# Gated graph layers by row halves, tiny VectorE operations with two tensors, and new durations for the merge

## The chip, the cores and the metric

The kernel runs on one core of a Trainium2 chip. The metric is the device time of one execution in microseconds (us). A run here is a median of several executions, taken on one chip together with executions of the kernel before. Views of the profile, and losses per period, come from one profiled execution of each kernel. A *ratio* is the mean time of one kernel's fast executions over that of the kernel before in the same rounds, so it is not quite the quotient of the two medians beside it.

## The reference, cut to what matters

`x` has shape (128, 64, 256): 128 graphs of 64 nodes. Four graph layers follow one another, each `x = layernorm(x + layer(x, adj))`. Two of them matter here.

```python
# layer 0: five gated steps
A = (adj != 0).astype(x.dtype)
for l in range(5):
    m = einsum('bnd,de->bne', h, weight[l])
    agg = einsum('bij,bid->bjd', A, m)
    h = gru_cell(agg, h, w_ih, w_hh, b_ih, b_hh)   # r, z, n; h' = (1-z)*n + z*h
# layer 2: norm and logarithm of each row, then the graph sum, then back onto the ball
n = clip(norm(x), 1e-15); x_tangent = arctanh(clip(n)) * x / n
support = einsum('bij,bjd->bid', adj, x_tangent)
out = project(tanh(norm(support)) * support / norm(support))
```

## The kernel before

The 128 graphs are 16 groups of 512 rows; three groups are in flight. Every operation is first *recorded* with an engine, a cost in us, what it writes and what it reads. A greedy merge then fixes the order in which the operations of the groups in flight are issued, so the order is static and depends on the recorded costs (`HOPS` is the time that it allows for a result to reach another engine):

```python
HOPS = {"from PE": 0.3, "to PE": 0.4, "else": 0.2}
def dve(n, run, w, r):  flow.op("DVE", 0.16 + 0.0011 * n, run, w, r)
def act(n, run, w, r):  flow.op("ACT", 0.16 + 0.001 * n, run, w, r)
def pool(us, run, w, r=()):  flow.op("POOL", us, run, w, r)
```

Each gated layer makes 512 x 256 products in two halves of 256 rows with fewer multiplications than the plain way. It needs four differences, t1 to t4, that GpSimd computes and that TensorE then multiplies by prepared weights:

```python
minus(t1, of(a, 1), of(a, 0), [a])                    # a is agg; of(a, n) is its half n
minus(t2, of(h, 1), lambda: view(t1), [(h, 1), t1])
minus(t3, of(h, 1), of(a, 1), [(h, 1), (a, 1)])
minus(t4, lambda: view(t2), of(h, 0), [t2, (h, 0)])
... # p_hn with 512 columns
product(p1, a11[l], k_of(a, 0), True, False, (a, 0))
act(512, copy of p1 to uu)                            # the "U copy"
product(p_in[0], ...); product(p1, a12, ...); tanh; new_n(0, ur)
product(pu, s2[l], k_view(t2), True, True, t2);  plus(uu, pu, uu)
product(pw, s1[l], k_view(t1), True, True, t1);  plus(uw, pw, uu)
product(pv, s3[l], k_view(t3), True, False, t3); plus(uz, pv, uw)
product(p4, s4[l], ...)
... # tanhs, p_in[1], new_n(1), then pv += na22 * t4, new_state(1), new_state(0)
```

`plus` is an addition on VectorE of a PSUM bank (pu, pv, pw and the other banks take the products' results) and an SBUF tile. In the profile t1 and t2 are the halves of tile tA, t3 and t4 those of tB; U, V, Z and R hold the sums, hT the state, and x_n is the layer norm's output, made from mv, ve and rstd. In layer 2 the norm's square root is a `pow` on GpSimd, the limits and the logarithm's argument `fac` are a chain of VectorE operations on 128x4, and `Ln` is on ScalarE.

## Time and profile before

| | before |
|---|---|
| time, median of 3 (range) | 2674.82 us (2669.52 to 2675.11) |
| TensorE busy | 93% of the span |
| matmul work at back-to-back spacing | 2405 us |
| steady period of a group | 159.2 us |
| of it lost on TensorE (gaps and slow matmuls) | 10.7 us |

The order repeats from group to group, so the steady period (start of one group's `ps_hid` to the next one's) is the thing to compare. A period's loss is the sum over its matmuls of the distance to the next matmul, less the distance that the same width has back to back (0.216 us at 256 columns).

### The profile page before, as it was taken

How to read it: one execution, taken by the hardware profiler on the slowest of the kernel's cores; microseconds unless marked ns; L12 is line 12 of the kernel's file. 1: busy time of each engine (PE TensorE's matmuls, PEld its weight loads, DVE VectorE, ACT ScalarE, POOL GpSimd, SP SyncE). 2: the span in 40 equal slices, each digit the busy share in tenths (PEclk: the TensorE clock that was granted, in tenths of full speed). 3: DMA queues.
4: the chain of work that ended last, by engine and by line, in shares of the span. 5: the costliest groups of instructions: out<-in, count | busy, mean ns of one | idle time of the engine just before them, and what ended most of it. 6: DMA issues, size and time to landing. Idle time of an engine off the chain costs nothing.

```text
span 2673.3 us, 31183 instructions
## 1 busy us (share of the span) xinstructions
PE 2491.5 (93%) x11330; PEld 1963.8 (73%) x11330; DVE 1606.5 (60%) x3593; ACT 1068.0 (40%) x2211; POOL 746.1 (28%) x707
## 2 busy tenths in 40 slices
PE   8999899999999999999999999999999999999874
PEld 5877777678677777877778687777877777777643
DVE  2456666466574756756476575646657575566635
ACT  2444343344343434434344443434434443433322
POOL 4232232322314132132413313232132413222220
PEclk9999999999999999999999999999999999999887
DMA  3000000000000000000000000000000000000000
GB/s 117 1 9 0 18 9 11 16 1 26 1 19 9 1 26 1 18 9 18 9 1 26 1 19 8 11 17 1 26 1 18 8 1 26 1 9 8 8 8 8
DMA packets 39144, 35.07 MB, mean 13 GB/s; under 512 B 9892, under 2 KB 38592, under 8 KB 38992
## 3 DMA queue, kind: packets, MB, share of 16 engines
q1 hardware_dynamic: 34848, 28.05, 3.4%
q10 hardware_dynamic: 3744, 4.46, 0.5%
q8 instruction: 90, 1.47, 0.2%
q0 software_dynamic: 400, 0.57, 0.1%
q14 instruction: 62, 0.51, 0.1%
HBM read 24.69 MB, written 8.39 MB: 12 GB/s over the span
## 4 chain that ended last, share of the span: by engine, by line
PE 49%; issue 19%; DVE 14%; POOL 13%; ACT 4%; DMA 0%; POOLq 0%; DVEq 0%; ACTq 0%
PE ps_o L222 8%; PE ps_hid L222 8%; PE p_r L480 7%; POOL tA L537 5%; PE p_v L480 4%; POOL tB L537 4%; PE p_hn L222 4%; PE ps_agg L222 3%; PE p_w L480 3%; PE p_in L480 3%; PE p_u L480 3%; POOL rstd L492 2%; PE ps_a L222 2%; DVE st L489 1%; DVE x_n L495 1%
## 5 line engine op out<-in xcount | busy, mean ns | idle before, releaser
L537 POOL TENSOR_TENSOR tA<-agg 128x512 f32<-128x512 f32 x80 | 107.3, 1341 | 900.3 <-ACT agg L474 620.3
L480 PE MATMUL p_in<-agg,w_in 128*128 128x256 f32 x1280 | 310.9, 382 | 0.0
L222 PE MATMUL p_hn<-hT,w_hn 128*128 128x512 f32 x640 | 306.6, 598 | 0.1
L480 PEld LDWEIGHTS p_in<-agg,w_in 128*128 128x128 f32 x1280 | 243.2, 192 | 31.8
L222 PE MATMUL ps_o<-w2s,hid 128*128 128x256 f32 x1024 | 231.0, 381 | 5.9 <-DVE hid L690 5.9
L222 PE MATMUL ps_hid<-aggm,w1s 128*128 128x512 f32 x512 | 224.6, 597 | 0.7 <-ACT aggm L474 0.7
L222 PEld LDWEIGHTS ps_o<-w2s,hid 128*128 128x128 f32 x1024 | 195.1, 191 | 40.8 <-DVE hid L690 7.9
L670 DVE TENSOR_TENSOR sqs<-sqs,sq 128x512 f32<-128x512 f32 x112 | 79.1, 706 | 225.0 <-POOL sq L667 224.7
L480 PE MATMUL p_r<-hT,a 128*128 128x256 f32 x640 | 176.5, 419 | 37.4 <-ACT U L601 37.4
L480 PEld LDWEIGHTS p_r<-hT,a 128*128 128x128 f32 x640 | 133.8, 212 | 69.7 <-ACT U L601 43.5
L222 PEld LDWEIGHTS ps_hid<-aggm,w1s 128*128 128x128 f32 x512 | 97.8, 192 | 118.1 <-issue 115.4
L561 ACT ACTIVATE hnb<-p_hn,half_b 128x512 f32<-128x512 f32 x160 | 109.7, 686 | 151.5 <-PE p_hn L222 151.4
L222 PEld LDWEIGHTS p_hn<-hT,w_hn 128*128 128x128 f32 x640 | 114.9, 192 | 74.3 <-issue 66.7
L583 DVE SCALAR_TENSOR_TENSOR R<-R,hnb 128x512 f32<-128x512 f32 x80 | 54.9, 686 | 190.2 <-ACT R L574 190.2
L480 PE MATMUL p_u<-tA,s 128*128 128x256 f32 x640 | 164.2, 391 | 0.0
L480 PE MATMUL p_r<-agg,a 128*128 128x256 f32 x640 | 157.5, 379 | 0.0
L480 PE MATMUL p_r<-hT,s 128*128 128x256 f32 x640 | 155.9, 379 | 0.0
L495 DVE TENSOR_SCALAR x_n<-y,mv,rstd 128x256 f32<-128x256 f32 x192 | 66.4, 408 | 148.6 <-POOL rstd L492 148.6
L480 PE MATMUL p_v<-tB,s 128*128 128x256 f32 x640 | 154.4, 381 | 0.0
L480 PEld LDWEIGHTS p_r<-agg,a 128*128 128x128 f32 x640 | 119.4, 190 | 47.5 <-issue 32.7
L480 PE MATMUL p_w<-tA,s 128*128 128x256 f32 x640 | 153.8, 379 | 0.0
L480 PE MATMUL p_v<-tB,na 128*128 128x256 f32 x640 | 153.8, 379 | 0.0
(179 smaller groups left out, 4837.2 us busy)
## 6 DMA issues: line engine op xcount, KB each, us to landing
x<-in_x_dram SPq DMA_DIRECT2D x16, 512.0 KB, 4.1
xr<-in_x_dram SPq DMA_DIRECT2D x16, 512.0 KB, 3.9
out_dram<-x_n SPq DMA_DIRECT2D x16, 512.0 KB, 2.9
edge<-in_adj_dram SPq DMA_DIRECT2D x32, 64.0 KB, 2.4
wm<-in_L_gnn_weight_dram ACTq DMA_DIRECT2D x5, 256.0 KB, 8.4
w1s<-in_L_gnn_W_dram ACTq DMA_DIRECT2D x1, 1024.0 KB, 11.5
w2s<-in_L_gnn_W_dram ACTq DMA_DIRECT2D x1, 1024.0 KB, 9.2
aw_in_L_gnn_w_ih_dram<-in_L_gnn_w_ih_dram ACTq DMA_DIRECT2D x1, 512.0 KB, 6.1
```

The lines of the kernel that those rows point to most:

```text
L222: nc.tensor.matmul(o, lhsT, rhs, start=(k == 0), stop=(k == nk - 1))
L480: pe(256, lambda c=c, k=k: nc.tensor.matmul(ps[:, c * HR:(c + 1) * HR], w[:, k, c * P:(c + 1) * P], v(k), start=first and c == k == 0, sto ...
L489: dve(256, lambda b=b: nc.vector.bn_stats(st[:, b, :], y[:, b, :]), [(st, b)], [(y, b)])
L492: pool(1.04, lambda: nc.gpsimd.tensor_tensor(rstd.tile(), ve.tile(), m_half, OP.pow), [rstd], [ve])
L495: dve(256, lambda b=b: nc.vector.tensor_scalar(o[:, b, :], y[:, b, :], mv[:, b, 0:1], rstd[:, b:b + 1], OP.subtract, OP.mult), [(o, b)], [ ...
L537: pool(1.04, lambda: nc.gpsimd.tensor_sub(view(o), x0(), x1()), [o], r)
L561: act(512, lambda ps=ps, c=c, hnb=hnb: nc.scalar.activation(hnb[:, c, :], ps.tile(), AF.Identity, bias=half_b[:, 2 * KD + c:2 * KD + c + 1 ...
L583: dve(512, lambda: nc.vector.scalar_tensor_tensor(t.tile(), t.tile(), 1.0, hnb[:, :, half(n)], OP.add, OP.mult), [t], [t, hnb])
L670: dve(512, lambda sq=sq: nc.vector.tensor_add(sqs.tile(), sqs.tile(), sq.tile()), [sqs], [sqs, sq])
```

## The change

The intent: half 0 of a gated layer should end early, the durations that the merge uses should be those of the trace, and tiny VectorE operations should escape waiting for GpSimd. Cut to the core:

```diff
-    HOPS = {"from PE": 0.3, "to PE": 0.4, "else": 0.2}
+    HOPS = {"from PE": 0.25, "to PE": 0.3, "else": 0.1}
-        flow.op("DVE", 0.16 + 0.0011 * n, run, w, r)
+        flow.op("DVE", 0.16 + 0.00105 * n, run, w, r)
-        flow.op("ACT", 0.16 + 0.001 * n, run, w, r)
+        flow.op("ACT", 0.27 + 0.00077 * n, run, w, r)
-                pool(1.04, lambda: nc.gpsimd.tensor_sub(view(o), x0(), x1()), [o], r)
+                pool(1.32, lambda: nc.gpsimd.tensor_sub(view(o), x0(), x1()), [o], r)
 ...
+            def sides(n):          # turn, aggregate and p_hn of half n
+                ...
+            sides(0)
             product(p1, a11[l], k_of(a, 0), True, False, (a, 0))
 ...
             new_n(0, ur)
+            sides(1)
+            minus(t1, ...); minus(t2, ...); minus(t3, ...); minus(t4, ...)
             product(pu, s2[l], k_view(t2), True, True, t2)
             plus(uu, pu, uu)
+            product(pv, s3[l], k_view(t3), True, False, t3)
+            plus(uv, pv, uu)
+            product(pw, s1[l], k_view(t1), True, False, t1)
+            product(pv, na22, k_view(t4), False, True, t4)
+            plus(uv, pw, uv)
+            plus(uz, pv, uu)
+            product(pw, s4[l], k_of(h, 1), False, True, (h, 1))
 ... # new_state(0) as soon as uz is there; half 1 last
-        dve(4, lambda: nc.vector.tensor_scalar(xn.tile(), xn.tile(), MIN_NORM, None, OP.max), [xn], [xn])
+        dve(4, lambda: nc.vector.scalar_tensor_tensor(xn.tile(), xn.tile(), MIN_NORM, xn.tile(), OP.max, OP.max), [xn], [xn])
 ... # eight more of this kind
```

So there are three parts: **tiny** (two tensors), **durations**, and **halves**.

More of the change, by code (lines that the diff above doesn't have):

```diff
@@ L275 @@
     nc.vector.memset(ones, 1.0)
+    one4 = const.tile([P, NB], F32, name="one4")
+    nc.vector.memset(one4, 1.0)
     p_half = const.tile([P, NB], F32, name="p_half")
@@ L395, in sums @@
                 flow.op(e, us, lambda o=o, x0=x0, x1=x1: v.tensor_sub(o.tile(), x0.tile(), x1.tile()), [o], [x0, x1])
-        sums("DVE", 0.7) if l == 0 else sums("POOL", 1.04)
+        sums("DVE", 0.7) if l == 0 else sums("POOL", 1.32)
     load(1)
@@ L521, in gated @@
             hr = rows("B", f"hr{l}") if l else xt
-            for n in range(2):
+            hnb = u("y", f"hnb{l}", (P, KD, R))
+            def sides(n):
                 if l:
                     ps = rows_of(h, n)
-                    act(512, lambda ps=ps, n=n: nc.scalar.copy(hr[:, 2 * n:2 * n + 2, :], blocks_of(ps.tile())),
+                    act(512, lambda: nc.scalar.copy(hr[:, 2 * n:2 * n + 2, :], blocks_of(ps.tile())),
                         [(hr, 2 * n), (hr, 2 * n + 1)], [ps])
                 aggregate(agg, hr, 2 * n, n)
+                p_hn = bank("p_hn")
+                product(p_hn, w_hn, lambda k: h[:, k, half(n)], True, True, (h, n))
+                for c in range(KD):
+                    act(300, lambda c=c: nc.scalar.activation(
+                        hnb[:, c, half(n)], p_hn[:, c * HR:(c + 1) * HR], AF.Identity,
+                        bias=half_b[:, 2 * KD + c:2 * KD + c + 1], scale=0.5), [(hnb, (n, c))], [p_hn, half_b])
             hN = u("h", f"hT{l}", (P, KD, R))
@@ L546, in k_view @@
                 return lambda k: t[0][:, t[1] * KD + k, :]
-            minus(t1, of(a, 1), of(a, 0), [a])
-            minus(t2, of(h, 1), lambda: view(t1), [(h, 1), t1])
-            minus(t3, of(h, 1), of(a, 1), [(h, 1), (a, 1)])
-            minus(t4, lambda: view(t2), of(h, 0), [t2, (h, 0)])
-            hnb = u("y", f"hnb{l}", (P, KD, R))
-            for c in range(KD):
-                ps = bank("p_hn")
-                for k in range(KD):
-                    pe(512, lambda ps=ps, c=c, k=k, h=h: matmul(
-                        ps.tile(), w_hn[:, k, c * P:(c + 1) * P], h[:, k, :], k, KD), [ps], [w_hn, h])
-                act(512, lambda ps=ps, c=c, hnb=hnb: nc.scalar.activation(
-                    hnb[:, c, :], ps.tile(), AF.Identity, bias=half_b[:, 2 * KD + c:2 * KD + c + 1], scale=0.5),
-                    [(hnb, c)], [ps, half_b])
-            p1, pu, pv, pw, p4 = bank("p_r0"), bank("p_u"), bank("p_v"), bank("p_w"), bank("p_r1")
+            p1, pu, pv, pw = bank("p_r0"), bank("p_u"), bank("p_v"), bank("p_w")
             p_in = [bank("p_in"), bank("p_in")]
-            uu, uw, uz, ur = (u(t, f"{t}_{l}", (P, KD, HR)) for t in "UVZR")
+            uu, uz, uv, ur = (u(t, f"{t}_{l}", (P, KD, HR)) for t in ("ZUVR" if l % 2 else "UZVR"))
             def plus(o, ps, x):
@@ L583, in new_n @@
                 dve(512, lambda: nc.vector.scalar_tensor_tensor(
-                    t.tile(), t.tile(), 1.0, hnb[:, :, half(n)], OP.add, OP.mult), [t], [t, hnb])
+                    t.tile(), t.tile(), 1.0, hnb[:, :, half(n)], OP.add, OP.mult), [t], [t, (hnb, (n, 0)), (hnb, (n, 1))])
                 dve(512, lambda: nc.vector.tensor_add(t.tile(), blocks_of(p_in[n].tile()), t.tile()), [t], [t, p_in[n]])
@@ L596, in new_state @@
                     hN[:, :, half(n)], hN[:, :, half(n)], 0.5, t.tile(), OP.mult, OP.add), [(hN, n)], [(hN, n), t])
+            sides(0)
             product(p1, a11[l], k_of(a, 0), True, False, (a, 0))
-            act(512, lambda: nc.scalar.copy(uu.tile(), blocks_of(p1.tile())), [uu], [p1])
+            act(420, lambda: nc.scalar.copy(uu.tile(), blocks_of(p1.tile())), [uu], [p1])
             product(p_in[0], w_in[l], k_of(a, 0), True, True, (a, 0))
@@ L605, in gated @@
             new_n(0, ur)
+            sides(1)
+            minus(t1, of(a, 1), of(a, 0), [a])
+            minus(t2, of(h, 1), lambda: view(t1), [(h, 1), t1])
+            minus(t3, of(h, 1), of(a, 1), [(h, 1), (a, 1)])
+            minus(t4, lambda: view(t2), of(h, 0), [t2, (h, 0)])
             product(pu, s2[l], k_view(t2), True, True, t2)
             plus(uu, pu, uu)
-            product(pw, s1[l], k_view(t1), True, True, t1)
-            plus(uw, pw, uu)
             product(pv, s3[l], k_view(t3), True, False, t3)
-            plus(uz, pv, uw)
-            product(p4, s4[l], k_of(h, 1), True, True, (h, 1))
-            plus(uw, p4, uw)
-            tanh_half(uw, inplace(uw), 0, uw)
+            plus(uv, pv, uu)
[4 more added lines that the diff above has]
+            product(pw, s4[l], k_of(h, 1), False, True, (h, 1))
             tanh_half(uz, inplace(uz), 1, uz)
+            new_state(0, ur, uz)
+            tanh_half(uv, inplace(uv), 1, uv)
+            plus(uu, pw, uu)
             product(p_in[1], w_in[l], k_of(a, 1), True, True, (a, 1))
-            new_n(1, uw)
-            product(pv, na22, k_view(t4), False, True, t4)
-            plus(uu, pv, uu)
-            tanh_half(uu, inplace(uu), 1, uu)
-            new_state(1, uw, uz)
-            new_state(0, ur, uu)
+            tanh_half(uu, inplace(uu), 0, uu)
+            new_n(1, uu)
+            new_state(1, uu, uv)
             return hN
@@ L714, in group @@
         pool(1.04, lambda: nc.gpsimd.tensor_tensor(xn.tile(), ss.tile(), p_half, OP.pow), [xn], [ss])
-        dve(4, lambda: nc.vector.tensor_scalar(xn.tile(), xn.tile(), MIN_NORM, None, OP.max), [xn], [xn])
+        dve(4, lambda: nc.vector.scalar_tensor_tensor(xn.tile(), xn.tile(), MIN_NORM, xn.tile(), OP.max, OP.max), [xn], [xn])
         dve(4, lambda: nc.vector.reciprocal(rn.tile(), xn.tile()), [rn], [xn])
-        dve(4, lambda: nc.vector.tensor_scalar(xn.tile(), xn.tile(), MAX_ARG, None, OP.min), [xn], [xn])
-        dve(4, lambda: nc.vector.tensor_scalar(fac.tile(), xn.tile(), -1.0, 1.0, OP.mult, OP.add), [fac], [xn])
+        dve(4, lambda: nc.vector.scalar_tensor_tensor(xn.tile(), xn.tile(), MAX_ARG, xn.tile(), OP.min, OP.min), [xn], [xn])
+        dve(4, lambda: nc.vector.scalar_tensor_tensor(fac.tile(), xn.tile(), -1.0, one4, OP.mult, OP.add), [fac], [xn])
         dve(4, lambda: nc.vector.reciprocal(fac.tile(), fac.tile()), [fac], [fac])
@@ L727, in series @@
             nc.vector.tensor_mul(n2.tile(), xn.tile(), xn.tile())
-            nc.vector.tensor_scalar(ser.tile(), n2.tile(), 1.0 / 13.0, None, OP.mult)
+            nc.vector.scalar_tensor_tensor(ser.tile(), n2.tile(), 1.0 / 13.0, one4, OP.mult, OP.mult)
             for q in (11, 9, 7, 5, 3):
                 nc.vector.scalar_tensor_tensor(ser.tile(), ser.tile(), 1.0 / q, n2.tile(), OP.add, OP.mult)
-            nc.vector.tensor_scalar(ser.tile(), ser.tile(), 1.0, None, OP.add)
-            nc.vector.tensor_scalar(near.tile(), xn.tile(), SERIES_BELOW, None, OP.is_lt)
+            nc.vector.tensor_add(ser.tile(), ser.tile(), one4)
+            nc.vector.scalar_tensor_tensor(near.tile(), xn.tile(), SERIES_BELOW, one4, OP.is_lt, OP.mult)
         dve(1250, series, [n2, ser, near], [xn])
@@ L754, in group @@
         pool(1.04, lambda: nc.gpsimd.tensor_tensor(un.tile(), us.tile(), p_half, OP.pow), [un], [us])
-        dve(4, lambda: nc.vector.tensor_scalar(unb.tile(), un.tile(), MIN_NORM, None, OP.max), [unb], [un])
+        dve(4, lambda: nc.vector.scalar_tensor_tensor(unb.tile(), un.tile(), MIN_NORM, un.tile(), OP.max, OP.max), [unb], [un])
         act(64, lambda: nc.scalar.activation(th.tile(), unb.tile(), AF.Tanh), [th], [unb])
@@ L761, in onto_ball @@
             nc.vector.tensor_mul(un.tile(), th.tile(), un.tile())
-            nc.vector.tensor_scalar(un.tile(), un.tile(), MIN_NORM, None, OP.max)
+            nc.vector.scalar_tensor_tensor(un.tile(), un.tile(), MIN_NORM, un.tile(), OP.max, OP.max)
             nc.vector.reciprocal(un.tile(), un.tile())
-            nc.vector.tensor_scalar(un.tile(), un.tile(), MAX_NORM, 1.0, OP.mult, OP.min)
+            nc.vector.scalar_tensor_tensor(un.tile(), un.tile(), MAX_NORM, one4, OP.mult, OP.min)
             nc.vector.tensor_mul(th.tile(), th.tile(), un.tile())
```

## The prediction

> **What bounds the kernel now.** I read the page's busy line and slices first, then the stretches table, then TensorE's timeline over two group periods, then the other engines' timelines where TensorE waited.
>
> The page, busy times and slices:
> ```profile
> PE 2491.5 (93%) x11330; PEld 1963.8 (73%) x11330; DVE 1606.5 (60%) x3593; ACT 1068.0 (40%) x2211; POOL 746.1 (28%) x707
> ...
> PE   8999899999999999999999999999999999999874
> ```
> TensorE is the bound from end to end; only the last slices fall off. How near is it to gapless? In the timeline back-to-back matmuls start 0.216 us apart at 256 columns, 0.430 at 512 and about 0.110 at 128. All 11330 records at these spacings make 2405 us. The first matmul starts at 10.8 us and the last ends at 2664.0, so 2664 - 10.8 - 2405 = 248 us are lost in between: 77 us after 2480, where fewer groups are left; about 29 before 480; some 140 in the 13 steady group periods of 160 us, 10.5 us each. No reordering can win more than the steady 140 us (5.2%) plus a part of the ends.
>
> Two stalls recur in every period. TensorE's timeline around each:
> ```profile
> 1052.64 1.89 PE L480 MATMUL p_in<-agg,w_in 128*128 128x256 f32 x8
> 1057.28 2.67 PE L480 MATMUL p_r<-hT,a 128*128 128x256 f32 x8 [2.74 <-ACT U L601]
> ...
> 991.06 1.46 PE L480 MATMUL p_in<-agg,w_in 128*128 128x256 f32 x6
> 995.59 2.45 PE L222 MATMUL ps_agg<-edge,x_n 128*128 128x128 f32 x16 [3.07 <-DVE x_n L495]
> ```
> Eight matmuls take 1.89 us, but 2.67 or more after the stall: matmuls come every 0.427 us for some 4 us before 0.216 returns. So the first stall costs 2.9 + 9 x 0.21 = 4.8 us, the second 3.2 + 1.3 = 4.5. With 0.8 us at ps_a and up to 0.9 at ps_hr that is the 10.5. Stalls of 0.9 us leave no slow matmuls behind, nor does one of 2.3 us at 479; one of 2.4 at 443 does.
>
> The second stall is a queue on GpSimd. Its timeline:
> ```profile
> 992.41 1.26 POOL L537 TENSOR_TENSOR tB<-tA,hT 128x512 f32<-128x512 f32 x1
> 993.64 0.23 POOL L491 TENSOR_SCALAR ve<-mv 128x4 f32<-128x4 f32 x1
> 993.96 1.04 POOL L492 TENSOR_TENSOR rstd<-ve,m_half 128x4 f32<-128x4 f32 x1
> ```
> The layer norm's mv was ready at 988.2; its ve stood behind eight subtractions of two groups. The first stall: ScalarE stands in Ln from 1050.8 to 1056.0, waiting for fac, and the copy U that TensorE needs stands behind it. fac is late because of tiny VectorE operations:
> ```profile
> 1050.86 1.22 DVE L715 TENSOR_SCALAR n<-n 128x4 f32<-128x4 f32 x1 [2.65 <-POOL n L714]
> 1052.12 0.18 DVE L716 RECIPROCAL rn<-n 128x4 f32<-128x4 f32 x1
> 1052.33 0.98 DVE L717 TENSOR_SCALAR n<-n 128x4 f32<-128x4 f32 x1
> ```
> The 1.22 and 0.98 end when GpSimd's current subtraction ends; in the last group, with GpSimd idle, the same lines take 0.17.
>
> **What the Trainium skill says.** "SBUF — State Buffer", SBUF: two separate sides: VectorE and GpSimd share one port pair, an exclusive lock, taken by a VectorE operation in a 2-port mode *or with two SBUF inputs*; the loser blocks. The trace agrees on both halves, and this matters, for the change gives the tiny operations two SBUF inputs. At 2484.7 GpSimd runs a subtraction:
> ```profile
> 2484.67 1.27 POOL L537 TENSOR_TENSOR tB<-tA,hT 128x512 f32<-128x512 f32 x1
> 2484.73 1.23 DVE L727 TENSOR_TENSOR n<-n 128x4 f32<-128x4 f32 x1
> 2485.88 0.16 DVE L732 TENSOR_SCALAR near<-n 128x4 int32<-128x4 f32 x1
> ```
> L727 has two tensor inputs and takes 1.23 instead of 0.15. Likewise L595 (two SBUF inputs, 128x512) takes about 1.75 us in the 19 cases that start inside a subtraction and 0.68 elsewhere. "TensorE: Matmul & The Clock Gate", Part 1: a window of about 3.4 us without work halves TensorE's clock until it has been busy that long. The trace agrees in kind; here gaps of 2.4 to 3.2 us already do it. "PSUM — Partial Sum Buffer", Engine vs sequencer instructions: ScalarE, VectorE and GpSimd queues are strict FIFO; the two stalls above are that.
>
> **The change part by part.**
>
> *p_hn by halves.* 4 matmul pairs of 512 columns a layer become 8 of 256: 8 x 0.430 = 3.44 us against 16 x 0.216 = 3.46. Over 80 layers +1.6 us. Weight loads (0.19 us each) fit under a 0.216 matmul. ScalarE's hnb goes from two of 0.686 to four of about 0.47, +0.5 us a layer, 40 us of an engine that is 40% busy: not on the path by itself.
>
> *Same products, same sums.* Nine products of 4 matmul pairs and five additions a layer, before and after. Total TensorE work is 2407 us.
>
> *Tiny operations.* Nine of a group's TENSOR_SCALARs get two tensors. If that escaped the lock, L715, L717, L719 and L728 would lose about 0.77 us each, fac would come 3.5 us sooner, and the first stall (16 x 4.8 = 77 us at most) would go. By L727 it does not escape; what decides is whether GpSimd is busy then. I count nothing for the replacement itself.
>
> *The new order* decides. I compared the built instruction orders of both kernels. First, both old stalls: the U copy now precedes Ln on ScalarE or belongs elsewhere, and at most one group's four subtractions stand before the layer norm's ve. With durations from the trace x_n arrives 1 to 2 us before its matmuls. Both stalls go: -9.3 us a group.
>
> Second, what it adds. The differences t1..t4 need both halves of agg. Before, all of half 0's products ran after agg: in the steady groups the order has 6.9 to 9.5 us of matmuls (counted at the spacings above) between the last ps_agg of layers 2 to 4 and p_u. Now half 1's agg comes after half 0's products, and mostly 3.9 to 5.8 us is left. p_u needs t2, the third subtraction: 0.2 hop + 0.58 copy + 3 x 1.22 + 0.15 = 4.6 us. So many layers stall by 0 to 0.7 us. In every second group (7, 9, 11, 13) layer 3 has only 1.3 us: a stall of 3.3 us, with slow matmuls 5.2.
>
> The order repeats every two groups. I followed the queues by hand through both kinds of period from the end of ps_o. Odd group under way: agg2's copy stands behind a Square that waits for x_n, so p_u waits 1.8; tan is 1.3 late; the copy of agg0 stands behind a Tanh, p_in waits 1.7; p_u of layer 0 0.7; small ones 0.7; layer 3 5.2. Sum 11.4 us. Even: p_r behind the same Square 1.1; x3T behind Tanhs 1.0; ps_e behind gated VectorE work 1.9; ps_T and layer 4 0.9. Sum 4.9 us. Mean 8.2, to which port blocking adds: GpSimd's fours now fall beside new_state and beside the tiny chain before y2, 1 to 3 us a group. New: about 10 us against 10.5.
>
> The ends: in the last group's layers half 1's chain (two Tanhs, five VectorE operations, 6 us) now follows the last matmul, where before 3.6 us were waited; earlier layers win about 2 each from the early half 0. Together -3 us. Sum: 13 x (10.0 - 10.5) - 3 + 1.6 = -8 us. I allow for some of my waits overlapping and take -15: 2660 us.
>
> **Rivals.** (1) *The old stalls go and little replaces them.* For it: VectorE and ScalarE are idle 40% and 60%, and the scheduler's GpSimd figure (1.32 instead of 1.04) now is close to the measured 1.27. Against: p_u's distance of 1.3 us is in the order. It would make 2674 - 13 x 6 - 5 = 2590 us. (2) *The tiny operations do escape the lock.* Against: L727. If GpSimd is idle in their place it hardly matters; where it is busy (before y2) it saves up to 2 us a group: 2635 us. (3) *More stalls cross the length that halves the clock.* Each costs about 2 us more; with two more a group +50 us: 2710 us. (4) *ScalarE becomes the wait*, having 42 more us and Ln in its queue: contained in my counts, else as (3).
>
> **Range and chances.** Of the hand-followed waits each may be off by 1 us, so a period by perhaps 3 us, 13 x 3 = 39 us around 2660, cut at the upper side by what the order still has to interleave: 2618 to 2704. Faster by over 2% (below 2621) needs rival 1 nearly in full: 0.15. Slower by over 2% (above 2728): 0.05. Within: 0.80.
>
> **What would show it.** Right, if TensorE's busy work is unchanged (11970 records, 640 more), waits for ACT U and for x_n at ps_agg have nearly gone, and p_u waits for GpSimd's tA in the odd groups with slow matmuls behind it, p_in for ACT agg. The tiny lines: 0.17 us where GpSimd is idle, over 1 us for two-tensor forms that start inside a subtraction. Wrong, if steady periods fall below 155 us (the added waits do not occur), or if two-tensor tiny operations stay at 0.17 beside a running subtraction.

## More of the kernel before

The waits in total, from the list of what TensorE waited for (columns: tile and line, what released it and its line, us in total, times, longest):

```profile
PE ps_agg L222 <- DVE x_n L495: 43.0, 15, 4.6
PE p_r L480 <- ACT U L601: 37.4, 14, 4.1
PE ps_hr L461 <- DVE hT L595: 22.0, 18, 4.9
```

The first two are the stalls that the prediction describes.

## The result, and the profile after

After: 2712.54 us median of 4 (2706.25 to 2713.96); before in the same rounds 2674.87. The ratio is 1.0141, with a 95% interval of 1.0120 to 1.0162. The change makes the kernel 38 us slower.

The page of the changed kernel, busy times and TensorE's slices:

```profile
PE 2488.3 (92%) x11970; PEld 2059.1 (76%) x11970; DVE 1675.7 (62%) x3594; ACT 1079.3 (40%) x2371; POOL 780.8 (29%) x707
...
PE   7999998999999899998999989999999999999874
```

There are 640 more matmul records, as expected, and no more TensorE work. VectorE is 69 us busier than before (1606.5) although it does the same operations (one constant is set in addition). What TensorE waited for:

```profile
PE p_u L482 <- POOL tA L550: 44.2, 37, 3.6
PE ps_hr L463 <- DVE hT L592: 27.4, 18, 4.5
PE p_v L482 <- DVE V L567: 24.8, 19, 4.2
PE ps_sup L222 <- DVE tan L743: 24.1, 7, 9.9
PE ps_agg L222 <- DVE x_n L497: 18.9, 16, 3.8
```

The wait for ACT's U is gone and that for x_n is more than halved. In their place stand p_u for GpSimd's tA and a second newcomer, p_v for VectorE's V. The longest p_u stall, in TensorE's timeline and then in GpSimd's (columns: start, us, engine and line, operation, out<-in, shapes, count; in brackets the idle time before it and its releaser):

```profile
1266.97 0.59 PE L482 MATMUL p_w<-tA,s 128*128 128x256 f32 x2
1271.19 3.37 PE L482 MATMUL p_u<-tA,s 128*128 128x256 f32 x8 [3.62 <-POOL tA L550]
```
```profile
1266.97 1.26 POOL L550 TENSOR_TENSOR tA<-agg 128x512 f32<-128x512 f32 x1 [18.56 <-DVE st L491]
1268.20 1.71 POOL L550 TENSOR_TENSOR tB<-hT,agg 128x512 f32<-128x512 f32 x1
1269.87 1.26 POOL L550 TENSOR_TENSOR tA<-hT,tA 128x512 f32<-128x512 f32 x1
```

Three subtractions end at 1271.1 and p_u starts. The eight p_u matmuls then take 3.37 us instead of 1.89: the slow clock. The same stall of 3.62 us comes four times; at 1596.70 and 1920.92 the eight matmuls after it took 1.99 us, so the slow clock does not always follow.

The newcomer, p_v, comes from a queue on VectorE. TensorE's stall and then VectorE's timeline ahead of it:

```profile
1403.90 3.58 PE L482 MATMUL p_v<-tB,na 128*128 128x256 f32 x8 [2.65 <-DVE V L567]
```
```profile
1395.81 1.62 DVE L586 TENSOR_TENSOR hT<-hT,R 128x512 f32<-128x512 f32 x1
1397.36 1.22 DVE L764 TENSOR_TENSOR th<-th,rn 128x4 f32<-128x4 f32 x1
...
1400.08 1.66 DVE L774 SCALAR_TENSOR_TENSOR y<-ps_sup,th,x_n 128x256 f32<-128x256 f32 x4
...
1403.18 0.66 DVE L567 TENSOR_TENSOR V<-p_v,U 128x512 f32<-128x512 f32 x1
```

The product by na22 adds into the bank p_v and so must wait until V has read it. V stands in VectorE's queue behind L586, which takes 1.62 us where 0.69 is usual, and L764, a 128x4 operation that takes 1.22 us instead of 0.16. Both started while GpSimd subtracted.

Per steady period (mean of eight periods, of 159.2 us before and 163.0 after; matmul work is 148.56 us in both), TensorE loses:

| us per period | before | after |
|---|---|---|
| ps_agg for x_n | 3.2 | 1.3 |
| p_r for U | 2.9 | 0 |
| p_u for tA | 0 | 4.0 |
| p_v for V | 0 | 3.0 |
| ps_hr for hT | 0.9 | 1.6 |
| p_in and p_r for agg | 0 | 1.3 |
| ps_agg for hnb | 0 | 0.7 |
| ps_a for x3T | 0.8 | 0.1 |
| matmuls at the slow clock | 3.0 | 2.3 |
| sum, with small ones | 10.7 | 14.4 |

### The profile page after: what moved, and what is told of

It is laid out like the page before. It is cut to its first block, busy times and chain, and to the rows that moved or that the text cites. A ratio compares the mean times of both kernels' runs of the same rounds, so it can differ in the third digit from the quotient of the medians.

```text
span 2704.5 us, 32558 instructions
## 1 busy us (share of the span) xinstructions
PE 2488.3 (92%) x11970; PEld 2059.1 (76%) x11970; DVE 1675.7 (62%) x3594; ACT 1079.3 (40%) x2371; POOL 780.8 (29%) x707
## 4 chain that ended last, share of the span: by engine, by line
PE 56%; DVE 21%; POOL 10%; issue 6%; ACT 6%; DMA 0%; POOLq 0%; DVEq 0%; ACTq 0%; SPq 0%
PE ps_hid L222 8%; PE p_v L482 7%; PE ps_o L222 7%; PE p_r L482 7%; PE p_w L482 5%; PE p_in L482 5%; POOL tA L550 4%; PE ps_agg L222 3%; PE p_hn L482 3%; POOL tB L550 3%; PE p_u L482 3%; DVE st L491 2%; PE ps_a L222 2%; DVE x_n L497 2%; DVE hT L590 2%
## 5 line engine op out<-in xcount | busy, mean ns | idle before, releaser
L482 PE MATMUL p_hn<-hT,w_hn 128*128 128x256 f32 x1280 | 323.6, 381 | 0.0
L482 PEld LDWEIGHTS p_hn<-hT,w_hn 128*128 128x128 f32 x1280 | 230.0, 192 | 23.7
L571 ACT ACTIVATE V<-V,half_b 128x256 f32<-128x256 f32 x160 | 73.2, 501 | 377.5 <-DVE V L567 377.5
L482 PE MATMUL p_v<-tB,na 128*128 128x256 f32 x640 | 163.9, 396 | 25.1 <-DVE V L567 24.8
L482 PEld LDWEIGHTS p_u<-tA,s 128*128 128x128 f32 x640 | 119.4, 194 | 78.1 <-POOL tA L550 60.9
L482 PEld LDWEIGHTS p_v<-tB,na 128*128 128x128 f32 x640 | 123.6, 198 | 50.4 <-DVE V L567 16.8
L482 PE MATMUL p_r<-hT,a 128*128 128x256 f32 x640 | 159.4, 379 | 0.0
L537 ACT ACTIVATE hnb<-p_hn,half_b 128x256 f32<-128x256 f32 x320 | 134.2, 469 | 62.5 <-PE p_hn L482 61.3
L482 PE MATMUL p_w<-hT,s 128*128 128x256 f32 x640 | 159.0, 380 | 0.0
L580 DVE SCALAR_TENSOR_TENSOR R<-R,hnb 128x512 f32<-128x512 f32 x80 | 65.0, 812 | 143.7 <-ACT R L571 143.3
```

What stands on the lines that cost most here:

```text
L482: pe(256, lambda c=c, k=k: nc.tensor.matmul(ps[:, c * HR:(c + 1) * HR], w[:, k, c * P:(c + 1) * P], v(k), start=first and c == k == 0, sto ...
L537: act(300, lambda c=c: nc.scalar.activation(hnb[:, c, half(n)], p_hn[:, c * HR:(c + 1) * HR], AF.Identity, bias=half_b[:, 2 * KD + c:2 * K ...
L571: act(256, lambda c=c: nc.scalar.activation(o[:, c, :], src(c), AF.Tanh, bias=half_b[:, i * KD + c:i * KD + c + 1], scale=0.5), [(o, c)], ...
L580: dve(512, lambda: nc.vector.scalar_tensor_tensor(t.tile(), t.tile(), 1.0, hnb[:, :, half(n)], OP.add, OP.mult), [t], [t, (hnb, (n, 0)), ( ...
```

## The experiments

My theory after the result: the halves' order leaves too little TensorE work between half 1's aggregate and the products of t1 to t4, so the subtractions' duration comes onto TensorE's path. Rivals: **A** the tiny two-tensor forms cause the loss; **B** the new durations do; **C** the tiny forms escape the lock and gain; **D** sums and states on VectorE (p_v, ps_hr) carry it by themselves; **E** the halved hn operations overload ScalarE. Eighteen kernels ran. Six of them (e9, e10, e11, e13, e17, e18) compute wrong results, to take away one cost.

### One part at a time: e1, e2, e3, e4, e12

e1 is the kernel before with the tiny part alone, e2 with the durations alone, e3 with the halves alone, e4 with halves and durations, e12 with durations and tiny. Their diffs are the parts of the diff above.

> The kernel before with only the tiny VectorE operations rewritten to two tensors; the order of instructions is that of the kernel before. My theory (the loss of 38 us comes from the gated order by halves): 2665 to 2685 us, no change beyond 0.4%, because the lines that stand beside a subtraction on GpSimd stay at about 1.2 us in the new form as in the old. Rival A (the tiny two-tensor forms cause the loss, by waiting for GpSimd's lock more often): 2700 us or more. Rival C (they escape the lock): 2600 to 2635 us, fac 3.5 us sooner and the wait for U gone.

> The kernel before with only the scheduler's durations changed. Its order keeps 7.8 us of matmuls or more between the last aggregate and p_u in nearly all layers. My theory: no new waits on p_u; the two old waits (U behind Ln, x_n behind subtractions) may shrink since the scheduler now knows what a subtraction takes: 2630 to 2680 us. Rival B (the new durations cause the loss): 2700 us or more.

> The kernel before with only the gated layers by row halves, the old durations. The order then has 1.7 to 4.3 us of matmuls between half 1's aggregate and p_u in most layers, where 4.6 are needed, less than in the changed kernel (3.9 to 5.8). My theory: at least as slow as the changed kernel, 2715 to 2770 us, with p_u's wait for tA above 44 us in sum. Rivals A and B (the loss comes from the tiny operations or the durations): 2680 us or less.

> The changed kernel without the tiny operations' rewriting: halves and durations together, the same order of instructions as the changed kernel. My theory: within 10 us of the changed kernel, 2703 to 2722 us. Rival A (the tiny forms cause the loss): 2680 us or less.

> The kernel before with the new durations and the tiny forms, without the gated layers by halves: the two parts that gained alone (ratios 0.9879 and 0.9979). If they add: 2630 to 2640 us, and this is the best of all versions so far.

| run | parts | median us | before, same rounds | ratio (95%) |
|---|---|---|---|---|
| e1 | tiny | 2668.27 | 2673.62 | 0.9979 (0.9963 to 0.9996) |
| e2 | durations | 2641.44 | 2673.62 | 0.9879 (0.9863 to 0.9894) |
| e3 | halves | 2724.91 | 2673.62 | 1.0194 (1.0179 to 1.0209) |
| e4 | halves, durations | 2716.74 | 2673.62 | 1.0160 (1.0144 to 1.0175) |
| e12 | durations, tiny | 2639.48 | 2674.04 | 0.9878 (0.9862 to 0.9895) |
| after | all three | 2712.54 | 2674.87 | 1.0141 (1.0120 to 1.0162) |

All five fell within what my theory said, though the tiny forms add nothing in e12 over e2. The halves are the loss, 75 us on top of the durations (e4 against e2). The durations alone are a gain of 32 us, and rivals A, B and C fall. In e1 TensorE's waits are those of the kernel before to within 0.6 us in every row that both have; its few us are fewer slow matmuls (56 against 64 us in sum, counting matmuls that come at over 1.5 times their usual distance with no wait in front), not a freed VectorE.

In e2 one of the two old stalls shrank and the other did not:

```profile
PE p_r L480 <- ACT U L601: 48.1, 15, 3.7
...
PE ps_agg L222 <- DVE x_n L495: 10.2, 16, 4.7
```

The merge that knows the subtraction's true length no longer sets eight of them before the layer norm's ve, and x_n's wait falls from 43 to 10 us.

### Restoring the distance: e5 and e6

e5 calls both `sides` first:

```diff
             sides(0)
+            sides(1)
             product(p1, a11[l], k_of(a, 0), True, False, (a, 0))
 ...
             new_n(0, ur)
-            sides(1)
```

e6 records the subtractions in the order in which the built program has them. Below the merge another layer moves t3 between the dependent t1 and t2, in both kernels; the merge does not know that.

```diff
             minus(t1, of(a, 1), of(a, 0), [a])
-            minus(t2, of(h, 1), lambda: view(t1), [(h, 1), t1])
             minus(t3, of(h, 1), of(a, 1), [(h, 1), (a, 1)])
+            minus(t2, of(h, 1), lambda: view(t1), [(h, 1), t1])
```

> The changed kernel with half 1's aggregate and hn side moved in front of half 0's products; all else (halves of hn, sums, tiny forms, durations) as in the changed kernel. The order then keeps 5.6 to 7.8 us of matmuls between half 1's aggregate and p_u in layers 2 to 4, over 20 in layers 0 and 1. My theory (too little work between the aggregate and the products of its differences): p_u's wait for tA falls from 44 us to under 8, and the time to 2635 to 2680 us. Rival D (the sums' waits on p_v and new_state's on ps_hr carry the loss, the distance does not matter): 2695 us or more. Rival E (halves of hn overload ScalarE): 2700 us or more, with the waits named ACT.

> The changed kernel with the four subtractions recorded in the order in which the built program has them (t1, t3, t2, t4), so that the merge places p_v's product before p_u's. The layer below the merge puts t3 between t1 and t2 in both. Distance to p_u 5.2 to 9 us in layers 1 to 4 (one layer 3.0), p_v 4 us or more where 3.4 are needed. My theory: p_u's wait falls to under 15 us in sum and the time to 2660 to 2695 us; the waits of p_v for V stay. If the distance does not matter: 2705 us or more.

e5: 2689.19 us, ratio 1.0059 (1.0044 to 1.0074). p_u's wait fell as expected, but the time missed my range by 9 us, because another stall of 5 us appeared in each period:

```profile
PE ps_sup L222 <- DVE tan L743: 73.5, 24, 9.9
...
PE p_u L482 <- POOL tA L550: 5.7, 2, 4.2
```

e6: 2735.71 us, ratio 1.0235 (1.0220 to 1.0251), a clear miss. p_u's wait is gone from the list, and p_v's has more than doubled:

```profile
PE p_v L482 <- DVE V L567: 55.4, 21, 6.6
```

So the distance decides p_u's wait, as I held, but not the time: each new static order brings its own set of stalls. Variants that are merged anew cannot settle the cause; the order must be kept.

### Two other places for the same wait: e11, e7, e8

e11 writes the product by na22 into p_w's bank (wrong result), with the same recorded reads and writes:

```diff
-            product(pv, na22, k_view(t4), False, True, t4)
+            product(pv, na22, k_view(t4), False, True, t4, pw)     # recorded as pv, written to pw
```

> The changed kernel with the product by na22 put into p_w's bank instead of p_v's (wrong result on purpose), so that it need not wait until VectorE has read p_v for V; the recorded order is the same, the layer below moves single matmuls. If that write-after-read wait costs on the path: p_v's 25 us of waits (19 times) go and the time falls by 15 to 30 us, to 2683 to 2698 us. If the wait is only covered by the next one (V late on VectorE makes p_w or Z late as well): 2703 to 2716 us.

2733.99 us, ratio 1.0233 (1.0218 to 1.0248): 21 us slower than the changed kernel. p_v's wait went and reappeared, longer, on p_w, which is read for V as well:

```profile
PE p_w L482 <- DVE V L567: 40.0, 17, 5.2
```

So another bank that is read for V does not remove the wait for V; a bank that V's sums do not read was not tried. (The layer below the merge also interleaved single matmuls differently, so the 21 us themselves are not explained.)

e7 is e12 with the U copy on VectorE, e8 the same with e6's order of subtractions:

```diff
-            act(512, lambda: nc.scalar.copy(uu.tile(), blocks_of(p1.tile())), [uu], [p1])
+            dve(512, lambda: nc.vector.tensor_copy(uu.tile(), blocks_of(p1.tile())), [uu], [p1])
```

> The kernel before with the tiny forms and the new durations, and the copy of U on VectorE instead of ScalarE (so it no longer stands behind Ln). The remaining stall of run e2 is p_r for ACT U (3.2 us and 1.7 us of slow matmuls in each period, 48 us of waits in all). If that stall is the queue behind Ln: 2575 to 2615 us. If VectorE's copy only stands behind the blocked tiny operations instead: 2620 to 2640 us.

> Run e7 with the subtractions recorded in their built order. In the old gated order p_u has 7 us of distance anyway, so my theory expects no gain from it: within 8 us of run e7. If the subtractions' place matters also there, 10 us or more apart.

e7: 2749.76 us, ratio 1.0288 (1.0271 to 1.0305); e8: 2765.69 us, ratio 1.0346 (1.0328 to 1.0365). Both expectations failed: e7 is 110 us slower than e12, and e8 is 16 us off e7. In e7 the wait for U became a wait for VectorE's U, three times as frequent:

```profile
PE p_r L482 <- DVE U L603: 122.7, 45, 4.7
```

VectorE's queue is in this kernel a worse place for something urgent than ScalarE's. Why e8 is 16 us above e7 I have not traced.

### The order kept, one cost taken away: e9, e10, e13, e17, e18

These five keep the recorded costs, so the merge gives the same order (in the traces e13's is equal on every engine; in e9 and e17 4 of 11970 matmuls and 37 of 3594 VectorE operations stand in another place, in e10 and e18 2 VectorE operations and no matmul).

e9 (changed kernel) and e10 (kernel before) cut the subtractions to 32 columns, which take about 0.3 us instead of 1.3 to 1.5. The matmuls read one column, broadcast.

```diff
-                pool(1.32, lambda: nc.gpsimd.tensor_sub(view(o), x0(), x1()), [o], r)
+                pool(1.32, lambda: nc.gpsimd.tensor_sub(view(o)[:, :, 0:16], x0()[:, :, 0:16], x1()[:, :, 0:16]), [o], r)
-                return lambda k: t[0][:, t[1] * KD + k, :]
+                return lambda k: t[0][:, t[1] * KD + k, 0:1].to_broadcast([P, HR])
```

> The changed kernel with GpSimd's four subtractions cut to 128x2x16 (wrong result on purpose; the matmuls read one column broadcast, TensorE's order is the same but for two rows). It takes away both what t2 costs on the way to p_u and the lock on VectorE, and nothing else. My theory (the loss lies in the subtractions' duration standing in a too short distance, and in their lock): p_u's wait falls from 44 us to under 5, VectorE's busy time by some 120 us, time 2570 to 2630 us, within 30 us of run e10. Rival D (the sums and states on VectorE carry the loss, with p_v for V and ps_hr for hT unchanged): 2650 us or more.

> The kernel before with the same cut of the subtractions (wrong result on purpose; TensorE's order the same). Here the x_n stall (ve behind eight subtractions) and the U stall (fac behind blocked tiny operations, Ln, U) should both go: 13 periods by 9.3 us are 121 us: 2545 to 2590 us. If either stall has another cause than the subtractions: 2600 us or more.

e9: 2558.23 us, ratio 0.9573 (0.9559 to 0.9587). e10: 2553.29 us, ratio 0.9558 (0.9542 to 0.9574). e9 came 12 us below its range. e10's gain of 121 us is what the two old stalls were worth by the prediction's count. The two kernels are now 5 us apart, and the changed kernel's p_u and p_v waits are both gone:

```profile
PE p_v L482 <- DVE V L567: 2.7, 7, 0.4
...
PE p_u L482 <- POOL tA L550: 2.4, 4, 0.6
```

This settles the main point: 33 of the 38 us between the kernels lie in the duration of GpSimd's subtractions. Sums, states and the halved hn operations stay as they were in e9, so by themselves they do not make the loss, and rivals D and E fall.

A long subtraction does two things: t2 is late (and GpSimd's queue is occupied), and VectorE is locked out meanwhile. e13 takes away the first alone: the subtractions run, but the products read half 1 of agg instead.

```diff
-                return lambda k: t[0][:, t[1] * KD + k, :]
+                return lambda k: a[:, k, half(1)]
```

> The changed kernel with the subtractions left as they are, but the products of t1 to t4 read half 1 of agg instead (wrong result on purpose; the order on every engine is the same). So nothing waits for the subtractions any more, while they still occupy GpSimd and still lock VectorE out. Run e9 took both away and gained 154 us. If the way from agg to t2 to p_u is most of it: 2570 to 2630 us. If the lock and the queue on GpSimd are most of it: 2640 to 2690 us; the wait of p_u for tA (44 us and little slow clock) then gives the difference to 2712.

e17 and e18 take away the second alone. The `pow` on 128x4 keeps GpSimd for 1.04 us, and in the trace before twelve VectorE operations with two SBUF inputs started beside one and took 0.69 us. So each subtraction became a `pow` and a cut subtraction:

```diff
-                pool(1.32, lambda: nc.gpsimd.tensor_sub(view(o), x0(), x1()), [o], r)
+                pool(1.32, lambda: (nc.gpsimd.tensor_tensor(view(o)[:, 0, 0:4], x0()[:, 0, 0:4], x1()[:, 0, 0:4], OP.pow),
+                                    nc.gpsimd.tensor_sub(view(o)[:, :, 0:16], x0()[:, :, 0:16], x1()[:, :, 0:16])), [o], r)
```

> The changed kernel with each subtraction replaced by a pow on 128x4 (1.04 us on GpSimd in the trace; VectorE operations with two SBUF inputs that start beside one take their usual 0.69 us) and the 128x2x16 subtraction of run e9 (wrong result on purpose). GpSimd is then as long busy and t2 as late as in the changed kernel, but VectorE is not locked out. If the lock makes the loss (as run e13 says: without the way to p_u the time stays at 2704): 2570 to 2625 us, with p_u's wait for tA still near 40 us. If lateness of t2 alone is enough: 2660 us or more.

> The kernel before with the same replacement; the order on TensorE is the same. Of the 121 us that run e10 gained, the U stall (tiny operations locked out: 13 x 4.8 = 62 us) should go, and the x_n stall (ve behind eight busy slots of GpSimd: 13 x 4.5 = 59 us) stay: 2600 to 2630 us, with the wait of ps_agg for x_n still near 43 us and that of p_r for U under 5 us. If both stalls come from the lock: 2550 to 2575 us.

| median us (loss per steady period) | changed kernel | kernel before |
|---|---|---|
| as it is | 2712.54 (14.4) | 2674.87 (10.7) |
| products do not wait, lock stays | e13: 2703.79 (15.5) | - |
| t2 as late, no lock | e17: 2653.60 (10.9) | e18: 2604.76 (5.7) |
| neither | e9: 2558.23 (3.1) | e10: 2553.29 (1.8) |

Ratios: e13 1.0106 (1.0086 to 1.0125), e17 0.9925 (0.9910 to 0.9940), e18 0.9741 (0.9725 to 0.9757).

e18 fell inside its range; e13 and e17 fell in neither of mine, e13 above both and e17 between them. That the lock was gone shows in e17 by an operation with two SBUF inputs that starts inside a pow, GpSimd's timeline and then VectorE's:

```profile
1246.08 1.01 POOL L550 TENSOR_TENSOR tA<-agg 128x4 f32<-128x4 f32 x1 [20.17 <-DVE st L491]
```
```profile
1246.45 0.66 DVE L586 TENSOR_TENSOR hT<-hT,R 128x512 f32<-128x512 f32 x1
```

Its waits keep p_u almost whole, and p_v for the most part; those of e13 have no p_u, but 1.7 times the p_v. e18 keeps the wait for x_n (43.0 before) and has none for U. First e17, then e13, then e18:

```profile
PE p_u L482 <- POOL tA L550: 38.3, 36, 3.2
...
PE p_v L482 <- DVE V L567: 17.0, 16, 3.3
```
```profile
PE p_v L482 <- DVE V L567: 43.3, 29, 4.4
PE ps_sup L222 <- DVE tan L743: 36.7, 8, 9.9
```
```profile
PE ps_agg L222 <- DVE x_n L495: 38.9, 15, 4.6
```

I read the medians so. With the lock taken away first, it costs either kernel about the same: 70 us before (2674.87 - 2604.76), 59 us after. Without it the two stand 49 us apart, without either effect 5. So along this path the lock is not what separates them. The late subtraction is: it costs 51 us before (2604.76 - 2553.29: the ve behind eight slots of GpSimd) and 95 us after (2653.60 - 2558.23). The other path gives other shares: in e13, with p_u's 44 us taken away and the lock kept, the time falls by 9, since V and tan, late through the lock, then make TensorE wait instead, and the lock would be worth the remaining 146. The kernel before has no run like e13, so what separates the two kernels along that path is not shown. The two effects stand side by side, and while the lock is there it hides most of what the lateness costs. (The losses in the table are of the profiled executions; that of the changed kernel was its fastest, 2706.25 us, that of e13 its slowest, 2704.76, so their two losses do not contradict the medians.)

### A version that beats both: e14, e15, e16

If the subtraction on GpSimd is the cost, VectorE may do it: its additions of this size take 0.69 us, and a subtraction in its own queue cannot lock its other operations out. e14 and e15 move all four (into e12 and into the changed kernel), e16 moves t1 and t2 only (into e12):

```diff
-                pool(1.32, lambda: nc.gpsimd.tensor_sub(view(o), x0(), x1()), [o], r)
+                dve(512, lambda: nc.vector.tensor_sub(view(o), x0(), x1()), [o], r)     # e16: where o is in tA
```

> Run e12 (durations and tiny forms, old gated order) with the four subtractions on VectorE, where an addition of this size takes 0.69 us: VectorE rises by about 220 us to some 1750 of 2600 (67%), and no subtraction locks it any more. If the lock is what the old order suffers from (U behind Ln behind the blocked tiny operations): 2560 to 2605 us. If a fuller VectorE queue puts new waits in its place: 2620 us or more.

> The changed kernel with the four subtractions on VectorE. The way to t2 is then 3 x 0.69 us instead of 3 x 1.27 us and the lock is gone, but the merge, knowing this, places p_u nearer (3 to 6 us) and VectorE is fuller. If the gated order by halves is only bad because of the slow subtraction: 2570 to 2620 us, near run e14. If its short distance stays bad: 2640 us or more, 40 above e14.

> Run e12 with t1 and t2 on VectorE and t3 and t4 on GpSimd. VectorE gets 110 us more and half of the lock stays. Between e12 and e14: 2590 to 2630 us if the lock counts; 2640 us or more if the lock's remaining half still hits the tiny operations of fac.

e14: 2592.95 us, ratio 0.9702 (0.9688 to 0.9717). e15: 2617.62 us, ratio 0.9788 (0.9772 to 0.9803). e16: 2584.83 us, ratio 0.9669 (0.9655 to 0.9684), all with correct results. e14 and e15 fell in their ranges (e15 by 2 us). e16 came 5 us below its own, as I had expected e14 to be ahead of it; why two on VectorE are better than four I have not traced. e16 beats the kernel before by 3.3%, of which the moved subtractions are 55 us against e12 (2639.48), or 2.1%. It keeps 5.1 us of loss a period; its page and its largest waits:

```profile
PE 2449.9 (95%) x11330; PEld 1932.0 (75%) x11330; DVE 1718.5 (67%) x3754; ACT 1068.0 (41%) x2211; POOL 558.5 (22%) x547
```
```profile
PE ps_hr L463 <- DVE hT L600: 24.5, 17, 4.0
PE p_r L482 <- ACT U L606: 21.5, 15, 2.2
```

The changed kernel gains as well when its subtractions move (95 us from 2712.54 to e15), but stays 25 us above e14.

## Why the prediction was wrong

The prediction said 2660 us, in 2618 to 2704; the kernel takes 2712.54. Its largest chance, within 2%, holds; the sign of the change does not.

- **No more TensorE work.** Right: 11970 records, and 148.56 us of matmul work a period in both kernels.
- **Tiny operations do not escape, and count for nothing.** Right. L719 takes 0.16 us with GpSimd idle (15 of 16 times) and 1.22 inside a subtraction; e1 alone moves the time by 0.2%.
- **Both old stalls go, -9.3 us a group.** Half right. The wait for U is gone. x_n keeps 1.3 of its 3.2 us a period, and the slow matmuls did not go with the stalls: 2.3 us against 3.0, behind other gaps now.
- **What the new order adds, by hand: a mean of 8.2 us.** Right in its main item: in layer 3 of every second group I had a stall of 3.3 us and 5.2 with slow matmuls; it is 3.62 of idle time, 3.78 by the distances. Slow matmuls followed it in two of the four cases (1.4 and 1.8 us), so 5.2 holds for the first and 4.6 is the mean. p_in for agg was put at 0.85 a period and measures 0.86. p_u as a whole measures 4.0 where mine make 2.9 without the slow matmuls. The waits at x3T and ps_e (1.5 us a period) hardly occur.
- **"To which port blocking adds: GpSimd's fours now fall beside new_state and beside the tiny chain before y2, 1 to 3 us a group. New: about 10 us against 10.5."** This is the step that failed. It measures 14.4 against 10.7. p_v for V (3.0), ps_hr for hT (1.6), x_n (1.3) and hnb (0.7) make 6.5 us a period that my hand count did not hold, and the allowance of 1 to 3 had to carry them all. e17, the same order without the lock, splits the error of 4.4 us. Without the lock a period loses 10.9 where the hand count had 8.2, and p_v for V (2.0) is most of that gap. The lock adds another 3.5 where the sum took about 1.8: with it p_v rises to 3.0, ps_hr from 0.4 to 1.6, and x_n and hnb come in. The direction was right, but I sized it by single blocked operations, while VectorE's busy time rose by 69 us, and by 138 us over e17.
- **Inside that step, a wait that I did not see at all.** In both programs the product by na22 must wait until VectorE has read p_v; now that read waits for U, and U for p_u's product, and only the product of s1 lies in between. In the kernel before, the products of s4 and w_in did. So p_u's lateness is passed on to p_v: p_v waits 17.0 us in e17, where the lock is gone, and 2.7 in e9, where the lateness is gone too.
- **The ends, -3 us.** Right in size, not in place: from 2470 us on it is about 6 us shorter, and about 4 us are lost before 845.
- **Rivals.** Rival 3, more stalls that halve the clock, gave a number near the result (2710) by luck, for a reason that does not hold: slow matmuls fell from 64 to 45 us in sum (counted as in e1). The waits in front of matmuls grew instead.
- **"I take -15: 2660 us."** The sum gave -8, and the other 7 had no term behind them. The range of 2618 to 2704 is also a little wider than the 39 us from which it was to come.

The sum, mended: eight steady periods are 30 us longer (159.2 to 163.0 each), nearly all of the 31 us between the two profiled executions (2673.3 and 2704.5; the medians are 38 apart).

What stays open: why e8 is 16 us slower than e7, what e11's 21 us are, what e13's cut would do to the kernel before, and how much of the 95 us between e17 and e9 is p_u itself and how much follows from it.

## What to carry to other kernels

Where a static merge decides the order, compare two variants only after fixing the order: keep the recorded costs, and take away one real cost at a time; otherwise every variant brings a new set of stalls. Take away two suspected costs one by one and together, for two that run side by side can each look small alone (9 and 59 us here, 154 together). And price an offloaded operation by what it locks and delays: subtractions of 1.3 us on an engine that is 28% busy cost 121 us of 2675, and moving half of them to the fuller engine gained 2.1% over e12.

## What the Trainium skill lacked or had wrong

- "SBUF — State Buffer", SBUF: two separate sides, has the lock held for the whole instruction by whichever of VectorE and GpSimd starts first, where the VectorE operation has two SBUF inputs and GpSimd's reads SBUF. The 128x512 subtractions agree (L586 with up to 1.80 us instead of 0.69, L764 with 1.22 instead of 0.16). GpSimd's `pow` on 128x4 does not: it reads SBUF and lasts 1.04 us, and two-input VectorE operations on 128x512 that start inside it take their usual time: 12 in the trace before, all 0.69 us, and 97 in e17, at most 0.78.
- The same section says what blocks, but not what it costs a tuned kernel: here 59 to 70 us of about 2700 while the lateness stays, and 121 to 154 us with the operation's own lateness.
- "TensorE: Matmul & The Clock Gate", Part 1, has the clock halve after an idle window of about 3.4 us in a free-running count. Here idle gaps of 2.65 and 3.62 us left 1.4 to 1.6 us of slow matmuls behind, and one of 2.68 us in the same two periods left none; nor did the 3.62 us at 1596.70 and 1920.92, or four of the twelve stalls of 3.07 us for x_n in the kernel before. So gaps well below 3.4 us can do it, and whether they do varies. In e1 the same waits as in the kernel before left 56 instead of 64 us of slow matmuls.
- "PSUM — Partial Sum Buffer" has no figure for what it costs when a product that adds into a bank again must wait for VectorE's read of that bank, and the read itself stands in a queue: 24.8 us in the changed kernel.
